# The E x E products of an attention and look-up feed-forward kernel, done by seven block products for eight

## The chip, the cores and the metric

The kernel runs on one core of one Trainium2 chip. The metric is the device time of one execution in microseconds (us), as the median of several runs. TensorE (PE) multiplies, VectorE (DVE) does elementwise work and the table look-ups, ScalarE (ACT) copies and does activations, GpSimd (POOL) and SyncE (SP) issue DMAs. Everything is fp32; one fp32 product appears in the trace as two MATMUL records, each with its weight load (PEld).

## The reference, cut to what matters

`x` is 2 x 2048 x 512, so there are B = 2 batches, S = 2048 tokens and E = 512 features.

```python
def attn(x, Wq, Wk, Wv, Wo):              # x is layer-normed
    q, k, v = x @ Wq, x @ Wk, x @ Wv
    qT, kT, vT = (swapaxes(t, 1, 2) for t in (q, k, v))   # b e s
    scores = einsum('bes,bfs->bef', qT, kT) / sqrt(16)    # 512 x 512 per batch
    o = einsum('bef,bfs->bes', softmax(scores), vT)
    return swapaxes(o, 1, 2) @ Wo

def ffn(x, lut, gate_idx, up_idx, down_idx):              # x is layer-normed
    gate, up = x @ lut[gate_idx].T, x @ lut[up_idx].T     # 1376 x 512 indices, 16 values
    return (silu(gate) * up) @ lut[down_idx].T

x = x + attn(layernorm(x), ...)
x = x + ffn(layernorm(x), ...)
```

The attention is over features, not tokens, so with n the normed tokens of a batch and G = n^T n (512 x 512), the scores are Wq^T G Wk / 4, and the output of the attention is n times M, where M = Wv A^T Wo and A is the softmax of the scores. Both G and M are 512 x 512 per batch.

## The kernel before, in words

The order of instructions on PE, ACT, DVE and SP is the order in which the program emits them; each engine's queue is worked off in that order, and an instruction that waits holds back all that were emitted after it on its engine. The program goes through these stages.

1. **Gram.** 8 chunks of 512 tokens (4 blocks of 128 each) are normed and multiplied into G of each batch (upper blocks only; `gram_mirror` fills the rest by PE transposes). Rows of n are stored in DRAM (`nd`), some here and some later (`n_stored`, one ACT pass and one DMA each).
2. **Eight E x E products.** For each batch: P1 = G Wk, scores S = Wq^T P1, softmax, T1 = A^T Wo, M = Wv T1. They come in the order p1_0, p1_1, s_0, s_1, t1_0, t1_1, m_0, m_1, where the last digit is the batch. `product` makes a result row block by row block: four blocks of 128 rows, each a bank of PSUM, filled by four products of 128 x 128 weights with 512 moving columns. ACT copies each bank out; for s, softmax runs on each row block by itself, with the maximum taken from PSUM on DVE and the exponent and the scaling by the reciprocal of the sum on ACT.
3. **y.** For each of 32 token blocks, `n_load` reads n back turned in 32 x 32 blocks, `n_turned` turns these blocks on DVE, `y_product` multiplies with M (4 products of 512 columns), and `side` adds the residual (DVE), takes the norm of the second layer (ACT), turns it by PE (`f_turned`) and, per two chunks, makes operand sums (`f_summed`).
4. **Gate and up** (`GateUp`): 11 blocks of 128 rows of weights by 4 pairs of chunks, each unit seven block products of Winograd's form (fourteen products of 512 columns).
5. **Down** (`Down`): 16 units of the same form with 256 moving columns.

The weights of stages 4 and 5 are looked up on DVE: a `Job` turns 128 x 1024 indices into values by some 20 steps of 0.4 to 1.3 us (bit tests, two-way choices with TENSOR_SCALAR, and COPY_PREDICATED). `gu0` to `gu10` are jobs for gate and up, `wd0` to `wd5` for down. The look-ups are spread over all other work by `pump(us)`, which emits so many us of steps (by the code's own costs, with a carried balance) at the place where it is called; the list `jobs` sets their order. A job `gu f` may start once unit f - 2 is through (its buffers come in twos).

Before, `pump` is called with 3.1 after each row block of p1, t1 and m, 2.2 in s, 0.3 in each y block and 0.8 between the products of stage 4. Tiles called `a0` to `a3`, `sq0`, `sq1` are 1 MB rooms that are reused: `a0` holds Wk, then Wo; `a1` holds Wq, then Wv^T.

Of the kernel before, what the change touches and what calls it, by code (L numbers as in the profile page):

```python
# [27 lines left out]

# [2 lines left out]

# [8 lines left out]
F32 = mybir.dt.float32  # L40
# [10 lines left out]
P = 128  # L51
H = 256
# [5 lines left out]
def tile_attn_ffn(  # L58
# [56 lines left out]
        return keep.tile([P, J, E], F32, tag=tag, name=name)  # L115

    wgu = tc.alloc_tile_pool(name="wgu", bufs=2)
    nlp = tc.alloc_tile_pool(name="nlp", bufs=1)
# [237 lines left out]
    def gram(c, j):  # L356
# [6 lines left out]
        for i in range(KB):  # L363
# [2 lines left out]
                start=c % CPB == 0 and j == 0, stop=c % CPB == CPB - 1 and j == J - 1,  # L366
            )

    gs = {}

    def gram_out(b):
# [38 lines left out]
    lut_pairs = lut_i.rearrange("p (k two) -> p k two", two=2)  # L410
    for c in range(1, NCH):
        for j in range(J):
            gram(c, j)
            if c + 1 < NCH and j < 2:
                for i in (2 * j, 2 * j + 1):
                    ln1[c + 1].stats(i, xc[c + 1][:, i, :])
                if j == 1:
                    ln1[c + 1].sqrt(0, J)
            elif c + 1 < NCH and j == 2:
                pump(0.6)  # L420
                ln1[c + 1].rest(0, J)
                pump(0.6)
            else:
                pump(1.9)
            if c == 1 and j == 2:
                nc.vector.tensor_tensor(
                    lut_x, lut_pairs[:, :, 0], lut_pairs[:, :, 1], ALU.bitwise_xor
                )
            if c == CPB and j == 1:
                gram_out(0)  # L430
            if c == CPB + 1 and j == 3:
                wk_sb = load_weight(wk, "a0", "wk_sb")
                wq_sb = load_weight(wq, "a1", "wq_sb")
            if c == CPB and j == 3:
                gram_mirror(0)

    def product(lhsT, rhs, name, by_slots=False):

        for m in range(KB):
            ps = bank(f"{name}_ps_{m}")  # L440
            for k in range(KB):
                cols = lhsT[:, k, m * P : (m + 1) * P]
                if by_slots:
                    cols = lhsT[:, k, :].rearrange("p (c m) -> p m c", m=KB)[:, m, :]
                nc.tensor.matmul(  # L445
                    ps, cols, rhs[:, k, :],
                    start=(k == 0), stop=(k == KB - 1),
                )
            yield m, ps

    def product_to(dest, lhsT, rhs, name, at=lambda m: None, by_slots=False):
        for m, ps in product(lhsT, rhs, name, by_slots):
            nc.scalar.copy(dest[:, m, :], ps)
            pump(3.1)
            at(m)
        return dest

    gram_out(1)
    to_store = iter([divmod(k, J) for k in range(STORED * J)])

    def n_stored(n=1):
        for c, j in itertools.islice(to_store, n):
            nc.sync.dma_start(nd[c, j], ln1[c].normed(j, xc[c][:, j, :]))

    p1 = [
        product_to(
            room("a2", "p1_0"), gs[0], wk_sb, "p1_0",
            lambda m: gram_mirror(1) if m == 1 else n_stored(),
        ),
        product_to(room("a3", "p1_1"), gs[1], wk_sb, "p1_1", lambda m: n_stored(1 + m % 2)),  # L470
    ]
    wo_sb = load_weight(wo, "a0", "wo_sb")
    att, last = [], None

    def softmax_end(a, m, sums, name):
        inv = small.tile([P, 1], F32, tag="inv", name=f"inv_{name}")
        nc.vector.reciprocal(inv, sums)
        nc.scalar.activation(a[:, m, :], a[:, m, :], AF.Copy, scale=inv)

    for b in range(B):  # L480
        a = room(f"sq{b}", f"a_{b}")
        for m, ps in product(wq_sb, p1[b], f"s_{b}"):
            pump(2.2)
            mx = small.tile([P, 1], F32, tag="mx", name=f"mx_{b}_{m}")
            nc.vector.reduce_max(mx, ps, axis=AX.X)
            nb = small.tile([P, 1], F32, tag="nb", name=f"nb_{b}_{m}")
            nc.vector.tensor_scalar_mul(nb, mx, -QK_SCALE)
            if last is not None:
                softmax_end(*last)
            sums = small.tile([P, 1], F32, tag="sums", name=f"sums_{b}_{m}")  # L490
            nc.scalar.activation(
                a[:, m, :], ps, AF.Exp, bias=nb, scale=QK_SCALE, accum_out=sums
            )
            last = a, m, sums, f"{b}_{m}"
            n_stored()
        att.append(a)
    pump(0.8)
    softmax_end(*last)
    wvT_sb = load_weight(wvT, "a1", "wvT_sb")
    t1 = [  # L500
        product_to(room(f"a{2 + b}", f"t1_{b}"), att[b], wo_sb, f"t1_{b}") for b in range(B)
    ]


    m_sb, nls, nTs, ys, xfs = [], {}, {}, {}, {}
    xb, xs = {}, {}

    def block(k):
        return xc[k // J][:, k % J, :]

    def n_load(h):

        if h < NBLK // 2:
            c, j = divmod(2 * h, J)
            nls[h] = nlp.tile([P, 2 * (P // Q), P], F32, tag="nl", name=f"nl_{h}", bufs=2)
            rows = nd[c, j : j + 2].rearrange("j (t b) e -> b (j t) e", b=Q)
            for i in range(KB):
                nc.sync.dma_start(nls[h][i * Q : (i + 1) * Q], rows[:, :, i * P : (i + 1) * P])

    def n_turned(k):  # L520

        if k < NBLK:
            n = P // Q
            nTs[k] = nlp.tile([P, KB, P], F32, tag="nT", name=f"nT_{k}", bufs=4)
            nc.vector.transpose(
                nTs[k].rearrange("p m (t b) -> p m t b", b=Q),
                nls[k // 2][:, n * (k % 2) : n * (k % 2) + n, :].rearrange(
                    "p t (a m) -> p m t a", a=Q
                ),
            )  # L530

    def y_product(k):
# [73 lines left out]
        if k % J == 0 and done in (1, 3):  # L606
            f_summed(done // 2)

    n_load(0)
    n_load(1)  # L610
    m_sb.append(product_to(room("sq0", "m_0"), wvT_sb, t1[0], "m_0", by_slots=True))
    m_sb.append(product_to(room("sq1", "m_1"), wvT_sb, t1[1], "m_1", by_slots=True))
    n_turned(0)
    n_turned(1)
    n_load(2)
# [9 lines left out]
    nlp.release()  # L625
    ffn = tc.alloc_tile_pool(name="ffn", bufs=1, reuse_waits="tile")


# [111 lines left out]
    def between():  # L740
        if todo:
            todo.pop(0)()
        else:
            pump(0.8)

    def tr(name):
        return psum("tr", name)
# [259 lines left out]
```

## Time and profile before

| | us |
|---|---|
| median of 3 runs | 1125.16 (1124.29 to 1125.23) |
| the profiled execution, device time | 1123.85 |
| its span, first to last instruction | 1121.8 |
| PE busy in the span | 1105.8 (99%) |
| DVE busy | 656.7 (59%) |
| ACT busy | 311.5 (28%) |
| the eight products, 80.26 to 190.78 | 110.5 |
| y, 190.78 to about 311 | 120 |
| gate and up, about 311 to 859 | 548 |
| down, 859 to the end | 263 |

The profiled execution is 2.05 us longer than its span; that remainder lies before the first and after the last instruction. The granted TensorE clock was 0.999. In the profile, a "group" is all instructions of one line, engine, operation and shape, with the total and the mean time of one; the chain is the sequence of work that ended last, followed back from the end. A mean duration of a MATMUL is longer than its share of PE's time, since matmuls overlap in the pipeline; PE's pace is read from the chain.

### The profile page before, as it was taken

Reading aid. Unit: us, or ns where it says so; the run is one execution under the profiler, and the core shown is the slowest. Engines: PE = TensorE matmul, PEld = TensorE weight load, DVE = VectorE, ACT = ScalarE, POOL = GpSimd, SP = SyncE. Lnnn points to the kernel's source line nnn. Section 1 sums busy time; section 2 is a strip of 40 time slices with the busy share of each in tenths; the row PEclk is TensorE's granted clock in tenths of the full one; section 3 lists DMA queues with packets and bytes.
Section 4 is the critical chain, followed back from the end, with each engine's and each line's share of the span. In section 5 each row is a group of like instructions: output and inputs, shape, how many; then the busy total and the mean of one; then the engine's idle time right before and its main releaser. Section 6 shows DMA issues by size and latency. Waiting matters only on the chain.

```text
span 1121.8 us, 9775 instructions
## 1 busy us (share of the span) xinstructions
PE 1105.8 (99%) x3388; PEld 630.4 (56%) x3388; DVE 656.7 (59%) x1191; ACT 311.5 (28%) x579; POOL 14.6 (1%) x31
## 2 busy tenths in 40 slices
PE   7999999999999999999999999999999999999998
PEld 4664446444444444444444444444437888888887
DVE  6896899566653847657566665856543344333341
ACT  4535622456562222222222222222221000000000
POOL 0000000000000000000000000000000000000000
PEclk9999999999999999999999999999999999999999
DMA  8253432444311111111211111111415453355420
GB/s 336 73 190 104 144 72 62 147 122 127 113 47 47 66 38 65 47 57 47 66 56 48 65 38 61 48 38 47 139 53 169 158 164 109 116 167 167 156 68 37
DMA packets 63232, 108.71 MB, mean 97 GB/s; under 512 B 5696, under 2 KB 22080, under 8 KB 61264
## 3 DMA queue, kind: packets, MB, share of 16 engines
q1 hardware_dynamic: 60992, 100.69, 26.6%
q0 software_dynamic: 2192, 7.41, 2.4%
q8 instruction: 26, 0.43, 0.2%
q14 instruction: 22, 0.18, 0.1%
HBM read 60.37 MB, written 47.71 MB: 96 GB/s over the span
## 4 chain that ended last, share of the span: by engine, by line
PE 98%; ACT 1%; DVE 0%; DMA 0%; issue 0%; ACTq 0%
PE a_g L637 27%; PE a_d L637 14%; PE c_g L637 13%; PE y L536 10%; PE c_d L637 7%; PE b_g L637 7%; PE gp L364 6%; PE b_d L637 4%; PE p_ps L445 2%; PE m_ps L445 2%; PE s_ps L445 2%; PE t_ps L445 2%; PE xt L560 1%; ACT xn_f L176 0%; DMA x<-in_x_dram 0%
## 5 line engine op out<-in xcount | busy, mean ns | idle before, releaser
L126 DVE TENSOR_TENSOR c<-c_g,u 128x512 f32<-128x512 f32 (+1 forms) x44 | 30.4, 690 | 178.3 <-PE c_g L637 178.3
L536 PE MATMUL y<-m,nT 128*128 128x512 f32 x256 | 114.0, 592 | 0.0
L637 PE MATMUL a_g<-xb,s 128*128 128x512 f32 (+1 forms) x176 | 82.8, 593 | 0.8 <-DVE c L126 0.8
L637 PE MATMUL a_g<-xT_a,s 128*128 128x512 f32 (+1 forms) x176 | 82.7, 592 | 0.0
L637 PE MATMUL a_g<-xb,w 128*128 128x512 f32 (+1 forms) x176 | 82.7, 592 | 0.0
L637 PE MATMUL c_g<-xb,w 128*128 128x512 f32 (+1 forms) x176 | 82.7, 592 | 0.0
L637 PE MATMUL b_g<-xb,w 128*128 128x512 f32 (+1 forms) x176 | 82.7, 592 | 0.0
L364 PE MATMUL gp<-xn_a 128*128 128x512 f32 (+3 forms) x256 | 71.2, 441 | 8.4 <-ACT xn_a L176 8.4
L536 PEld LDWEIGHTS y<-m,nT 128*128 128x128 f32 x256 | 46.8, 190 | 49.6 <-issue 49.5
L689 ACT ACTIVATE h<-h 128x512 f32<-128x512 f32 (+1 forms) x44 | 27.7, 630 | 156.9 <-DVE h L126 156.9
L364 PEld LDWEIGHTS gp<-xn_a 128*128 128x128 f32 x256 | 44.5, 193 | 34.9 <-issue 16.5
L637 PE MATMUL a_g<-xT_sq,s 128*128 128x512 f32 (+1 forms) x132 | 62.0, 592 | 0.0
L223 DVE TENSOR_SCALAR gu<-idx_gu,lut_x,lut_sb 128x1024 int32<-128x1024 int32 (+1 forms) x77 | 59.6, 790 | 0.0
L637 PEld LDWEIGHTS a_g<-xb,s 128*128 128x128 f32 (+1 forms) x176 | 32.9, 188 | 43.7 <-issue 37.7
L235 DVE COPY_PREDICATED gu<-b_gu,gu 128x1024 f32<-128x1024 int16 (+1 forms) x44 | 56.4, 1283 | 0.8
L637 PEld LDWEIGHTS b_g<-xb,w 128*128 128x128 f32 (+1 forms) x176 | 32.9, 188 | 42.0 <-issue 42.0
L637 PEld LDWEIGHTS c_g<-xb,w 128*128 128x128 f32 (+1 forms) x176 | 32.9, 188 | 41.6 <-issue 41.6
L637 PEld LDWEIGHTS a_g<-xb,w 128*128 128x128 f32 (+1 forms) x176 | 32.9, 188 | 41.5 <-issue 41.5
L637 PEld LDWEIGHTS a_g<-xT_a,s 128*128 128x128 f32 (+1 forms) x176 | 32.9, 188 | 41.5 <-issue 41.5
L637 PE MATMUL a_d<-dT,hs_a 128*128 128x256 f32 x224 | 56.2, 379 | 0.0
L235 DVE COPY_PREDICATED wd<-b_wd,wd 128x1024 f32<-128x1024 int16 (+1 forms) x42 | 51.1, 1217 | 1.1
L666 ACT COPY p<-a_g 128x512 f32<-128x512 f32 (+1 forms) x44 | 25.8, 586 | 84.1 <-PE a_g L637 84.1
(144 smaller groups left out, 1664.3 us busy)
## 6 DMA issues: line engine op xcount, KB each, us to landing
hd<-h SPq DMA_DIRECT2D x80, 256.0 KB, 2.0
h<-hd SPq DMA_DIRECT2D x40, 512.0 KB, 6.4
nd<-xn_a SPq DMA_DIRECT2D x32, 256.0 KB, 2.0
nl<-nd SPq DMA_DIRECT2D x64, 128.0 KB, 3.3
x1d<-x SPq DMA_DIRECT2D x8, 1024.0 KB, 4.1
r<-x1d SPq DMA_DIRECT2D x32, 256.0 KB, 4.2
out_dram<-r SPq DMA_DIRECT2D x32, 256.0 KB, 2.5
x<-in_x_dram SPq DMA_DIRECT2D x7, 1024.0 KB, 13.9
```

Source lines behind the costliest of these rows:

```text
L126: nc.vector.tensor_tensor(dest, a, b, ALU.add)
L223: vec.tensor_scalar(dest.bitcast(I32), idx, lut_x[:rows, k : k + 1], lut_i[:rows, at : at + 1], ALU.bitwise_and, ALU.bitwise_xor,)
L235: vec.copy_predicated(dest, masks[level - 1], t)
L364: nc.tensor.matmul(gp[b][i][:, i * P :], xn[:, i * P : (i + 1) * P], xn[:, i * P :], start=c % CPB == 0 and j == 0, stop=c % CPB == CPB - ...
L445: nc.tensor.matmul(ps, cols, rhs[:, k, :], start=(k == 0), stop=(k == KB - 1),)
L536: nc.tensor.matmul(ys[k], nTs[k][:, i, :], m[:, i, :], start=(i == 0), stop=(i == KB - 1))
L560: nc.tensor.transpose(ps[:, i * P : (i + 1) * P], xfs[k][:, i * P : (i + 1) * P], ident)
L637: nc.tensor.matmul(ps, lhsT, rhs, start=first and i == 0, stop=i == len(pairs) - 1, skip_group_check=not first,)
L666: nc.scalar.copy(self.p1, self.a)
L689: nc.scalar.activation(self.h0, self.h0, AF.Silu)
```

## The change

Each E x E product is now made by `Square`: the operands are cut into 2 x 2 blocks of 256 x 256, and the four result blocks come from seven block products in seven stages (in the order in which they are emitted: 11x11, S3xT3, S2xT2, 22xT4, S1xT1, 12x21, S4x22). A block product is 2 x 2 products of 128 x 128 weights by 256 moving columns; its two blocks of rows share one bank. Banks `u` (stages 0, 2, 4, 6) and `v` (stages 1, 3) are read out in the middle of their accumulation: stage 2 goes on adding to `u` after ACT has copied stage 0's sum, and so on. `left` and `right` give the four sums of an operand (one in place, three in new 256 KB tiles of the pool `sums`, ten in rotation), each one DVE operation of 128 x 512. `square` calls, after each stage, what the table `beside` lists for it, and then `pump(0.6)`.

The softmax runs on two row blocks at a time and reads the scores from SBUF. Wv^T is loaded by 16 DMAs that put its columns into another order, so that the weights of m are read without a stride; `n_load` now loads one block with four DMAs of 64 KB (before: two blocks with four DMAs of 128 KB), four blocks ahead, and takes its tiles, as `n_turned` does, from `sums` (before: from a pool of their own). Two places in Gram where `pump(1.9)` stood do the four sums of g_0 and of Wk instead. The order of look-up jobs changes, `pump` in y goes from 0.3 to 1.0, and in gate and up from 0.8 to 0.9.

```diff
-    jobs = [gu_job(0), gu_job(1)]
-    jobs += [down_job(i) for i in range(NPAIR + 1)]
-    jobs += [gu_job(f) for f in range(2, NFT)]
+    jobs = [gu_job(0), gu_job(1)] + [down_job(i) for i in range(NPAIR - 1)]
+    jobs += [gu_job(2), gu_job(3), down_job(NPAIR - 1), gu_job(4), gu_job(5), down_job(NPAIR)]
+    jobs += [gu_job(f) for f in range(6, NFT)]
...
+    def left(t, name, order=("S2", "S4", "S1")):
+        a11, a21 = t[:, 0:2, :H], t[:, 0:2, H:]
+        a12, a22 = t[:, 2:4, :H], t[:, 2:4, H:]
+
+        def s3():
+            for tag in order:
+                o.new(tag)
+            sub(a21, a11, a21)
+            o.update({"11": a11, "12": a12, "22": a22, "S3": a21})
+
+        o = Operand(name, [
+            s3, lambda: sub(o["S2"], a22, a21), lambda: sub(o["S4"], a12, o["S2"]),
+            lambda: add(o["S1"], o["S2"], a11),
+        ])
+        return o
...
+    class Square:
...
+        def mm(self, ps, a, b, first):
+            for m in range(2):
+                for k in range(2):
+
+                    nc.tensor.matmul(
+                        ps[:, m, :], self.a[a][:, k, m * P : (m + 1) * P], self.b[b][:, k, :],
+                        start=first and m == k == 0, stop=k == 1,
+                        skip_group_check=not (first and m == 0),
+                    )
...
+        def stages(self):
+            u = self.view("ea")
+            self.mm(u, "11", "11", True)
+            nc.scalar.copy(self.c11, u)
+            yield
+            v = self.view("ec")
+            self.mm(v, "S3", "T3", True)
+            nc.scalar.copy(self.c22, v)
+            yield
+            self.mm(u, "S2", "T2", False)
+            nc.scalar.copy(self.c21, u)
+            yield
+            self.mm(v, "22", "T4", False)
+            add(self.c21, v, self.c21)
+            yield
+            self.mm(u, "S1", "T1", False)
+            add(self.c22, u, self.c22)
+            yield
+            w = self.view("eb")
+            self.mm(w, "12", "21", True)
+            add(self.c11, w, self.c11)
+            yield
+            self.mm(u, "S4", "22", False)
+            nc.scalar.copy(self.c12, u)
+            yield
+
+    def square(a, b, dest, name, beside):
+
+        for i, _ in enumerate(Square(a, b, dest, name).stages()):
+            for op in beside.get(i, ()):
+                op()
+            pump(0.6)
...
+        def exp(self, h):
+            r = slice(2 * h, 2 * h + 2)
+            nc.vector.reduce_max(self.mx[:, r], self.a[:, r, :], axis=AX.X)
+            nc.vector.tensor_scalar_mul(self.nb[:, r], self.mx[:, r], -QK_SCALE)
+            for m in range(2 * h, 2 * h + 2):
+                nc.scalar.activation(
+                    self.a[:, m, :], self.a[:, m, :], AF.Exp, bias=self.nb[:, m : m + 1],
+                    scale=QK_SCALE, accum_out=self.sum[:, m : m + 1],
                 )
...
+        def end(self, h):
+            r = slice(2 * h, 2 * h + 2)
+            nc.vector.reciprocal(self.inv[:, r], self.sum[:, r])
+            for m in range(2 * h, 2 * h + 2):
+                nc.scalar.activation(
+                    self.a[:, m, :], self.a[:, m, :], AF.Copy, scale=self.inv[:, m : m + 1]
+                )
...
+    square(g[0], wk_ops, p1[0], "p1_0", {
+        1: [lambda: gram_mirror(1)], 2: [n_stored], 3: [n_stored], 4: g[1].todo[:2], 5: g[1].todo[2:],
+        6: [n_stored],
+    })
+    square(g[1], wk_ops, p1[1], "p1_1", {
+        0: [n_stored], 1: [n_stored], 2: wq_ops.todo[:2], 3: wq_ops.todo[2:],
+        4: [*p1_ops[0].todo[:2], n_stored], 5: p1_ops[0].todo[2:], 6: [n_stored],
+    })
...
+    square(wq_ops, p1_ops[0], att[0], "s_0", {
+        0: [n_stored], 1: [n_stored], 2: [*p1_ops[1].todo[:2], n_stored],
+        3: [*p1_ops[1].todo[2:], n_stored], 4: [lambda: soft[0].exp(1)],
+        5: [lambda: soft[0].end(1)], 6: [n_stored],
+    })
+    square(wq_ops, p1_ops[1], att[1], "s_1", {
+        0: [lambda: soft[0].exp(0)], 1: [lambda: soft[0].end(0)], 2: [n_stored],
+        3: [*wo_ops.todo[:2], n_stored], 4: [*wo_ops.todo[2:], lambda: soft[1].exp(1)],
+        5: [*att_ops[0].todo[:2], lambda: soft[1].end(1)], 6: att_ops[0].todo[2:],
+    })
+
+    wvT_sb = room("a1", "wvT_sb")
+    for k in range(KB):
+        for i in range(KB):
+            nc.sync.dma_start(
+                wvT_sb[:, k, :].rearrange("p (m c) -> p m c", m=KB)[:, :, i * Q : (i + 1) * Q],
+                wvT[k * P : (k + 1) * P, i * P : (i + 1) * P].rearrange("p (m a) -> p m a", a=Q),
             )
...
+    square(att_ops[0], wo_ops, t1[0], "t1_0", {
+        0: [lambda: soft[1].exp(0)], 1: [lambda: soft[1].end(0)], 2: att_ops[1].todo[:2],
+        3: att_ops[1].todo[2:], 4: [n_stored], 5: [n_stored],
+    })
+    square(att_ops[1], wo_ops, t1[1], "t1_1", {
+        3: wv_ops.todo[:2], 4: [*wv_ops.todo[2:], t1_ops[0].todo[0]], 5: t1_ops[0].todo[1:],
+    })
...
+    square(wv_ops, t1_ops[0], m_sb[0], "m_0", {2: t1_ops[1].todo[:2], 3: t1_ops[1].todo[2:]})
+    square(wv_ops, t1_ops[1], m_sb[1], "m_1", {
+        0: [lambda: n_load(0)], 3: [lambda: n_turned(0), lambda: n_load(1)],
+        6: [lambda: n_turned(1), lambda: n_load(2), lambda: n_load(3)],
+    })
     for k in range(NBLK):
         n_turned(k + 2)
-        if k % 2:
-            n_load((k + 1) // 2 + 2)
+        n_load(k + 4)
         y_product(k)
         if k >= 1:
             side(k, bank)
-        pump(0.3)
+        pump(1.0)
...
-            pump(0.8)
+            pump(0.9)
```

`right` is like `left`: T3 in place, then T2, T4 and T1, one DVE operation each.

More of the change, by code (lines that the diff above doesn't have):

```diff
@@ L31 @@
-import itertools
 from contextlib import ExitStack
@@ L117, in tile_attn_ffn @@
     wgu = tc.alloc_tile_pool(name="wgu", bufs=2)
-    nlp = tc.alloc_tile_pool(name="nlp", bufs=1)
+    sums = tc.alloc_tile_pool(name="sums", bufs=10)
     gub = tc.alloc_tile_pool(name="gub", bufs=1, side="right")
@@ L367, in gram, with __init__, new, right @@
             )
+    class Operand(dict):
+        def __init__(self, name, todo):
+            self.name, self.todo = name, [lambda op=op: op() for op in todo]
+        def new(self, tag):
+            self[tag] = sums.tile([P, 2, H], F32, tag="e", name=f"{tag}_{self.name}")
+            return self[tag]
+    def left(t, name, order=("S2", "S4", "S1")):
[11 more added lines that the diff above has]
+        return o
+    def right(t, name, order=("T2", "T4", "T1")):
+        b11, b12 = t[:, 0:2, :H], t[:, 0:2, H:]
+        b21, b22 = t[:, 2:4, :H], t[:, 2:4, H:]
+        def t3():
+            for tag in order:
+                o.new(tag)
+            sub(b12, b22, b12)
+            o.update({"11": b11, "21": b21, "22": b22, "T3": b12})
+        o = Operand(name, [
+            t3, lambda: add(o["T2"], b12, b11), lambda: sub(o["T4"], b21, o["T2"]),
+            lambda: sub(o["T1"], b22, o["T2"]),
+        ])
+        return o
     gs = {}
@@ L410, in tile_attn_ffn @@
     lut_pairs = lut_i.rearrange("p (k two) -> p k two", two=2)
+    ahead = []
     for c in range(1, NCH):
@@ L422, in tile_attn_ffn @@
                 pump(0.6)
+            elif ahead:
+                for op in ahead[:4]:
+                    op()
+                del ahead[:4]
             else:
@@ L433, in tile_attn_ffn @@
                 wq_sb = load_weight(wq, "a1", "wq_sb")
+                wk_ops = right(wk_sb, "wk")
+                ahead += wk_ops.todo
             if c == CPB and j == 3:
                 gram_mirror(0)
[L437 to L447, printed above, removed]
-                )
-            yield m, ps
@@ L451, in product_to @@
[L451 to L456, printed above, removed]
-    gram_out(1)
[L459 to L471, printed above, removed]
@@ L472, in tile_attn_ffn @@
-    wo_sb = load_weight(wo, "a0", "wo_sb")
[L473 to L492, printed above, removed]
-            )
-            last = a, m, sums, f"{b}_{m}"
-            n_stored()
-        att.append(a)
@@ L497, in tile_attn_ffn, with __init__, view @@
-    pump(0.8)
[L498 to L505, printed above, removed]
+                g_ops = [left(gs[0], "g_0")]
+                ahead += g_ops[0].todo
+    class Square:
+        def __init__(self, a, b, dest, name):
+            self.a, self.b, self.name = a, b, name
+            self.c11, self.c12 = dest[:, 0:2, :H], dest[:, 0:2, H:]
+            self.c21, self.c22 = dest[:, 2:4, :H], dest[:, 2:4, H:]
+        def mm(self, ps, a, b, first):
[6 more added lines that the diff above has]
+                    )
+        def view(self, tag):
+            return bank(f"{tag}_{self.name}").rearrange("p (m h) -> p m h", m=2)
+        def stages(self):
[23 more added lines that the diff above has]
+            yield
@@ new lines, in square, with n_stored, __init__, cols @@
+    def square(a, b, dest, name, beside):
+        for i, _ in enumerate(Square(a, b, dest, name).stages()):
+            for op in beside.get(i, ()):
+                op()
+            pump(0.6)
+    to_store = iter([divmod(k, J) for k in range(STORED * J)])
+    def n_stored():
+        c, j = next(to_store)
+        nc.sync.dma_start(nd[c, j], ln1[c].normed(j, xc[c][:, j, :]))
+    class Softmax:
+        def __init__(self, a, name):
+            self.a, self.name = a, name
+            def cols(tag):
+                return small.tile([P, KB], F32, tag=tag, name=f"{tag}_{name}")
+            self.mx, self.nb, self.sum, self.inv = (cols(t) for t in ("mx", "nb", "sum", "inv"))
+        def exp(self, h):
[6 more added lines that the diff above has]
+                    scale=QK_SCALE, accum_out=self.sum[:, m : m + 1],
+                )
+        def end(self, h):
[5 more added lines that the diff above has]
+                )
@@ new lines, in tile_attn_ffn @@
+    gram_out(1)
+    g = [g_ops[0], left(gs[1], "g_1")]
+    wq_ops = left(wq_sb, "wq", ("S2", "S1", "S4"))
+    p1 = [room(f"a{2 + b}", f"p1_{b}") for b in range(B)]
+    p1_ops = [right(p1[b], f"p1_{b}") for b in range(B)]
+    assert not ahead
+    square(g[0], wk_ops, p1[0], "p1_0", {
[6 more added lines that the diff above has]
+    })
@@ new lines, in tile_attn_ffn @@
+    wo_sb = load_weight(wo, "a0", "wo_sb")
+    wo_ops = right(wo_sb, "wo")
+    att = [room(f"sq{b}", f"a_{b}") for b in range(B)]
+    soft = [Softmax(att[b], f"{b}") for b in range(B)]
+    att_ops = [left(att[b], f"att_{b}", ("S1", "S2", "S4")) for b in range(B)]
+    square(wq_ops, p1_ops[0], att[0], "s_0", {
[3 more added lines that the diff above has]
+    })
@@ new lines, in tile_attn_ffn @@
+    wv_ops = left(wvT_sb, "wv", ("S2", "S1", "S4"))
+    t1 = [room(f"a{2 + b}", f"t1_{b}") for b in range(B)]
+    t1_ops = [right(t1[b], f"t1_{b}", ("T1", "T2", "T4")) for b in range(B)]
+    square(att_ops[0], wo_ops, t1[0], "t1_0", {
[5 more added lines that the diff above has]
+    })
@@ L506, in tile_attn_ffn @@
+    nls, nTs, ys, xfs = {}, {}, {}, {}
     xb, xs = {}, {}
@@ L509, in block, with n_load @@
         return xc[k // J][:, k % J, :]
[L511 to L516, printed above, removed]
+    def n_load(k):
+        if k < NBLK:
+            c, j = divmod(k, J)
+            nls[k] = sums.tile([P, P // Q, P], F32, tag="e", name=f"nl_{k}")
+            rows = nd[c, j].rearrange("(t b) e -> b t e", b=Q)
             for i in range(KB):
-                nc.sync.dma_start(nls[h][i * Q : (i + 1) * Q], rows[:, :, i * P : (i + 1) * P])
+                nc.sync.dma_start(nls[k][i * Q : (i + 1) * Q], rows[:, :, i * P : (i + 1) * P])
     def n_turned(k):
         if k < NBLK:
-            n = P // Q
-            nTs[k] = nlp.tile([P, KB, P], F32, tag="nT", name=f"nT_{k}", bufs=4)
+            nTs[k] = sums.tile([P, KB, P], F32, tag="e", name=f"nT_{k}")
             nc.vector.transpose(
                 nTs[k].rearrange("p m (t b) -> p m t b", b=Q),
-                nls[k // 2][:, n * (k % 2) : n * (k % 2) + n, :].rearrange(
-                    "p t (a m) -> p m t a", a=Q
-                ),
+                nls[k].rearrange("p t (m a) -> p m t a", a=Q),
             )
@@ L607, in side @@
             f_summed(done // 2)
[L609 to L615, printed above, removed]
+    m_sb = [room(f"sq{b}", f"m_{b}") for b in range(B)]
+    square(wv_ops, t1_ops[0], m_sb[0], "m_0", {2: t1_ops[1].todo[:2], 3: t1_ops[1].todo[2:]})
[3 more added lines that the diff above has]
+    })
     for k in range(NBLK):
         n_turned(k + 2)
-        if k % 2:
-            n_load((k + 1) // 2 + 2)
+        n_load(k + 4)
         y_product(k)
@@ L622, in tile_attn_ffn @@
             side(k, bank)
-        pump(0.3)
+        pump(1.0)
     pps.release()
-    nlp.release()
+    sums.release()
     ffn = tc.alloc_tile_pool(name="ffn", bufs=1, reuse_waits="tile")
@@ L743, in between @@
         else:
-            pump(0.8)
+            pump(0.9)
     def tr(name):
```

## The prediction

> **What bounds the kernel now.** I read first the page's busy times, then the chain in order of time, then windows over the eight products, then the groups by shape.
>
> ```profile
> PE 1105.8 (99%) x3388; PEld 630.4 (56%) x3388; DVE 656.7 (59%) x1191; ACT 311.5 (28%) x579; POOL 14.6 (1%) x31
> ```
>
> PE is never idle for long, so only less PE time, or new waits of PE, can move the end. The chain gives PE's pace (start, length, count of records):
>
> ```profile
> 80.26 6.87 PE p_ps L445 x16
> 87.13 0.66 PE gt L383 x6
> 87.78 20.60 PE p_ps L445 x48
> 108.38 27.47 PE s_ps L445 x64
> 135.85 27.47 PE t_ps L445 x64
> 163.32 27.47 PE m_ps L445 x64
> 865.93 4.75 PE a_d L637 x22
> ```
>
> The eight products are one unbroken run from 80.26 to 190.8. A record with 512 columns takes 27.47 / 64 = 0.429 us; one with 256 columns (last row, the down stage) takes 4.75 / 22 = 0.216 us. The windows over p1, s, t1 and m (columns: PE, PEld, DVE, ACT, POOL busy) show what else is there:
>
> ```profile
> 80.30:108.40 28.10, 28.10 (x71) 12.76 (x70) 19.03 (x24) 12.11 (x21) 0.72 (x1) 1.00 0.26 86
> 108.40:135.80 27.40, 27.40 (x65) 12.09 (x65) 21.11 (x38) 18.27 (x32) 0.72 (x1) 1.00 0.39 134
> 135.80:163.30 27.50, 27.50 (x66) 12.31 (x65) 26.79 (x35) 7.16 (x12) 0.72 (x1) 1.00 0.45 111
> 163.30:190.80 27.50, 27.50 (x66) 19.64 (x65) 27.12 (x31) 6.15 (x10) 1.65 (x3) 1.00 0.09 27
> ```
>
> DVE is full in the last two rows, with look-ups that nobody waits for. After the change work that PE does wait for goes into the same queue.
>
> **What is removed on PE.** A product is 16 matmuls, 32 records: 32 x 0.429 = 13.73 us. Seven block products are 28 matmuls, 56 records of 256 columns: 56 x 0.216 = 12.09 us. Eight times 1.64 is 13.1 us. This needs the weight load to stay hidden behind 0.216 us:
>
> ```profile
> L637 PE MATMUL a_d<-dT,hs_a 128*128 128x256 f32 x224 | 56.2, 379 | 0.0
> L637 PEld LDWEIGHTS a_d<-dT,hs_a 128*128 128x128 f32 x224 | 42.4, 189 | 6.0
> L445 PEld LDWEIGHTS m_ps<-t,wvT_sb 128*128 128x128 f32 x64 | 19.7, 308 | 7.9 <-issue 0.2
> ```
>
> The down stage loads 128 x 128 weights in 189 ns beside matmuls paced at 216 ns, and 16 units of it run without a gap; the new products have the same shape. The strided load of m (308 ns) would not fit, and the new order of Wv^T's columns takes that stride away. [...]
>
> **What is added on DVE and ACT.** In the eight products, at the spacing of back-to-back operations (a 128x512 add lasts 0.68 and the next starts 0.60 to 0.61 later):
> 40 operand sums (the eight of g_0 and Wk lie in Gram, in place of 3.8 us of look-ups): 40 x 0.605 = 24.2 us.
> 24 additions from PSUM (three a product): 24 x 0.61 = 14.6 us.
> Four maxima of 128x1024: the 128x512 one is 0.69, and adds of 512 and 1024 elements (0.68, 1.22) say 0.53 more, 1.22 each, with negation 1.4: 5.5 us.
> Look-ups: 56 x 0.6 = 33.6 us of the code's cost, times 1.045 (a job `wd` costs 16.6 by the code and 17.3 by the rows): 35.1 us. Before it was 92.8.
>
> With two transposes this is 81.6 us, against 96.7 us of PE: it fits on the whole, but it comes in bunches, and the leash is short. Before, a late DVE or ACT had eight banks of slack. Now stage 4 may not start on `u` before ACT copied stage 2, stage 6 not before DVE's `add(c22)` of stage 4, stage 3 not before ACT copied stage 1: one stage, 8 x 0.216 = 1.73 us, of slack each time.
>
> **The dense stretch.** From DVE's addition in stage 3 of s_1 to its `add(c22)` in stage 4 of t1_0, on which stage 6 waits, DVE gets: five additions (3.1), four sums of Wo, four of att_0, four of att_1 (12 x 0.605 = 7.3), two maxima with negation (2.8), eight pumps (5.0): 18.2 us. PE has nine stages there, 15.5 us. So 2.7 us are missing even if DVE never waits. It does wait: the reciprocal of a softmax half stands behind its two exponents on ACT (0.67 us and a read of the sum, 0.68 apart, so 1.4), and ACT's scalings stand ahead of the copies that free `u` and `v`. In t1_0, stages 0 and 1, only one pump step of about 0.6 covers this, so 1 us more; and a step of 1.3 us (COPY_PREDICATED) just ahead of a wanted addition, seen from PE, costs half of itself twice: 1.3 us. I take 5 us here. From s_0 to s_1 the other halves meet less DVE work, but ACT has five `n_stored` of 0.8 us, the table load for the exponent (1.28 us, idle-hidden before) and the scalings: 1.2 us. In p1_1, t1_1, m_0 and m_1 two sums and a look-up step stand ahead of `add(c22)`: about 0.45 us each, 1.8. Sum 8.0 us. The lower bound is the 2.7 us of pure shortage. The upper one takes each mean duration in full instead of the spacing (20.1 us in the stretch, 4.6 missing, two waits of 1.7, so 8.0), 2 us for s, and 0.7 for each of six lesser products: 14 us, all of the gain. I take 8.0, nearer the middle, because the rows show DVE's operations overlapping at their ends.
>
> **What is moved.** Look-ups leave the products (59.2 us of cost) and Gram (3.8), and 22.4 go to y. In y, PE needs 3.87 us a block (3.44 for y, 0.43 for the turn), DVE 1.1 (transpose) + 0.77 (residual) + 0.25 (norm) + 1.05 = 3.2: it fits, and the transpose runs two blocks ahead of its product, so that the 4.9 us of `f_summed` at blocks 16 and 24 find slack. The last 40.6 go to gate and up, where `pump(0.9)` allows 25.2 per block of weights and a job costs 18.3, so the rest is worked off in about six blocks. DVE's window there:
>
> ```profile
> 427.00:475.00 48.00, 48.00 (x114) 21.21 (x113) 30.31 (x44) 12.89 (x21) 1.06 (x2) 1.00 0.16 54
> ```
>
> 30.3 of 48 us become about 39; the additions there have at least two stages (3.4 us) of slack, so 0. Only at block 4 are some 2 us of steps issued in one go, since wd4 stands before gu4; the products already in PE's queue cover it. If that cover is gone it costs those 2 us. POOL's index loads follow the jobs and are hundreds of us early. The start of y: tile nT_1 needs a load that SP can issue only after stage 4 of m_1, because its room holds a sum of Wv until then; 4 issues of 0.45 and 3.3 to land, then 1.1, end about 3 us after m_1, and y_1 starts 3.4 after it. Just in time; I put 0.5 us there. The 16 passes of `n_stored` stay 16. `n_load`'s 64 more issues (0.45 each, 1.8 a block of 3.87) have room on SP; the x1d stores behind them are early.
>
> **The load of Wv^T.** 16 DMAs with 128-byte pieces, 8192 of them, issued when stage 5 of s_1 has read Wq's room, wanted by DVE in stage 3 of t1_1: 1.7 + 12.1 + 5 + 6.9 = 25.7 us later, and the stage after it covers some 1.7 more. No row shows 128-byte pieces.
>
> ```profile
> nl<-nd SPq DMA_DIRECT2D x64, 128.0 KB, 3.3
> wvT_sb<-in_wvT_dram SPq DMA_DIRECT2D x1, 1024.0 KB, 7.0
> ```
>
> The low bound is the plain load, 7.0. `nl` has 256 pieces of 512 bytes a DMA, issued every 0.45 us (median) to 1.28 (longest): 1.8 to 5.0 ns a piece, so 14.4 to 41 us, and 3.3 to land: 18 to 44. I take 18, the median row: hidden. [...]
>
> **The sum.** 1123.85 (profiled) - 13.1 + 8.0 + 0.5 = 1119.25. The profiled execution lies 1.3 us under the median, so the median to come is 1125.16 - 4.6 = **1120.6**. A difference under 0.2% (2.25 us) I count as none.
>
> **The rivals.**
> *DVE keeps up* (0.12): the waits overlap and only the shortage of 2.7 us stays: 1125.16 - 13.1 + 2.7 + 0.5 = 1115.3. For it: DVE's 81.6 us are 84% of PE's 96.7. Against: the bunch in s_1 and t1_0.
> *DVE and ACT give it all back* (0.16): 14 us of waits, 1126.6; with 11 and more it is no difference. For it: every softmax half is a chain DVE, ACT, DVE, ACT in queues that also hold the copies.
> *Wv^T comes late* (0.22, slower): one mechanism. It decides from 27.4 us after its issue; each us more holds DVE in t1_1, with `add(c22)` behind it, and PE in stage 6. From 34 us on the kernel is slower by over 0.2%; at 40 us it is 1120.6 + 12.6 = 1133.2. For it: the bound of 44 us, and that no row shows such pieces. Against: the median row.
> That 256-column products don't run at 0.216 us I leave out: 16 units of the down stage show them.
>
> **How the numbers follow.** The forecast, 5 to 10.8 us of waits (1117.6 to 1122.9), has 0.50. Faster is this and the first rival, 0.62; same is the second, 0.16; slower the third, 0.22. The range from 1115.0 to 1130.0 leaves out half of the first rival's lower side (0.05) and half of the third (0.11).
>
> **What would show it.** Right: 448 records of 256 columns in place of 256 of 512, p1 at about 25 us a pair with the turns, PE waits on DVE and ACT of 8 us, most in s_1 and t1_0; y from about 186; DVE above 80% busy in the products and about 39 of 48 us in the early blocks of gate and up, with no wait of PE there. Wrong: PE idle in t1_1 behind a DMA; waits spread evenly over all eight products; a pace other than 0.216; PE waiting in y or in gate and up.

## The result, and the profile after

The changed kernel takes 1121.16 us (median of 6 runs, 1119.73 to 1121.98); the one before takes 1125.04 in the runs beside it. The ratio is 0.9966, 95% interval 0.9954 to 0.9979, so 0.34% faster; the forecast was 1120.6.

The profiled execution took 1121.98 us with a span of 1119.9. It is a poor match for the one of before (1123.85, faster than all six of that kernel's runs in the comparison): the two differ by 1.9 us, the medians by 3.9. Most of the reason stands in the first 16 us, whose code is the same; it comes up again at the end. What follows is therefore read stage by stage. Busy times of the page first:

```profile
PE 1098.1 (98%) x3580; PEld 660.4 (59%) x3580; DVE 683.8 (61%) x1251; ACT 315.4 (28%) x587; POOL 14.7 (1%) x31
```

PE is busy 7.7 us less, and DVE, which has the operand sums and the additions to do, 27 us more. The windows over the pairs p1, s, t1 and m (columns as before: length, then PE, PEld, DVE, ACT, POOL busy with counts, PE's clock, DMA):

```profile
81.52:107.01 25.49, 25.10 (x120) 21.81 (x119) 15.02 (x22) 10.55 (x20) 0.00 (x0) 1.00 0.17 63
107.01:132.43 25.42, 24.71 (x113) 21.05 (x112) 20.65 (x34) 16.81 (x29) 0.73 (x1) 1.00 0.42 147
132.43:162.80 30.37, 26.90 (x113) 22.14 (x112) 22.22 (x36) 12.22 (x23) 0.00 (x0) 0.94 0.26 51
162.80:187.63 24.83, 24.44 (x113) 21.20 (x112) 18.86 (x28) 4.69 (x8) 0.72 (x1) 1.00 0.27 74
```

The lengths add up to 106.1 us, 4.4 less than before (110.5). A pair without any wait would take 24.2 (56 x 2 records of 0.216), and m comes within 0.7 of it; p1 has 0.66 us of transposes inside. t1 takes 30.4, and PE's clock there is 0.94. PE's records in order of time show t1_0 from its first stage on (start, length, what; in brackets the idle time named and what ended it; eight records at pace are 1.73 us apart from start to start):

```profile
132.43 1.89 PE L499 MATMUL ea_t<-wo_sb,a 128*128 128x256 f32 x8
134.61 1.97 PE L499 MATMUL ec_t<-wo_sb,a 128*128 128x256 f32 x8 [0.29 <-DVE a L122]
137.64 1.99 PE L499 MATMUL ea_t<-T_wo,S_att 128*128 128x256 f32 x8 [1.07 <-ACT t L511]
141.70 2.56 PE L499 MATMUL ec_t<-T_wo,a 128*128 128x256 f32 x8 [2.07 <-ACT t L515]
144.05 3.06 PE L499 MATMUL ea_t<-T_wo,S_att 128*128 128x256 f32 x8
146.95 1.89 PE L499 MATMUL eb_t<-wo_sb,a 128*128 128x256 f32 x8
```

Stage 1 waits for DVE's sum of att_0, stage 2 for ACT's copy of stage 0, stage 3 for ACT's copy of stage 1. The starts of stages 1 to 5 are late against the pace by 0.45, 1.30, 2.33, 0.62 and 1.17 us, 5.9 in all. The last two have no wait in front of them: 0.10 of the 0.62 is PE's restart (behind waits after which the matmuls are not slow, the next start comes 1.83 us later for 1.73: 105.18 to 107.01 in p1_1 behind 0.39 us, 125.42 to 127.25 in s_1 behind 0.36, 173.72 to 175.55 in m_0 behind 0.39), and the rest is matmuls that are slow themselves. The chain shows what stood before the longest wait (start, length, engine, what):

```profile
135.59 0.72 DVE wd L222
136.31 0.60 DVE S_att L122
136.91 0.60 DVE S_att L125
137.51 0.72 DVE wd L222
138.24 1.14 DVE mx L560
...
139.40 0.18 DVE nb L561
...
139.66 1.52 ACT a L563 x4
141.18 0.48 ACT t L515
...
141.70 1.35 PE ec_t L499 x5
```

The maximum of the softmax's second half belongs to stage 0 of t1_0 (over at 134.3), but DVE comes to it at 138.24, behind two look-up steps and two sums. Its input is late as well: ACT's last copy of s_1 ends at 137.1, because it stands behind scalings that waited for DVE's reciprocal of 135.19. ACT can do the exponents only after the maximum, and the copy that PE wants (L515) stands behind these. DVE's shortage reaches PE through ACT. And PE's clock in the windows around it (length, PE busy, clock):

```profile
134.00:141.70 7.70, 4.28 (x18) 1.00 0.68 108
141.70:143.00 1.30, 1.30 (x6) 1.00 0.00 0
143.00:146.00 3.00, 3.00 (x9) 0.50 0.35 129
```

PE was busy 4.28 of 7.70 us, and from 143 on, with work in hand, its granted clock is 0.50 for 3.4 us (0.80 between 146 and 147). That costs 0.57 us on stage 3's records (2.56 in the chain, for the 1.99 of eight records behind a wait at full clock) and 1.12 on stage 4's (2.85 for 1.73): 1.7 in all. Waits and restarts make up the other 4.2 of the 5.9.

After the products nothing is slower up to the first block of weights: y takes 120.85 us to the first product of gate and up, 120.84 before. In gate and up DVE is busier, as foreseen (a window of 48 us, in it 36.99 of DVE where before it had 30.31):

```profile
423.50:471.50 48.00, 48.00 (x113) 21.24 (x112) 36.99 (x52) 13.76 (x22) 2.15 (x4) 1.00 0.18 64
```

There is one wait, at the start of weight block 4, in PE's records in order of time:

```profile
507.67 1.98 PE L752 MATMUL c_g<-xb,w 128*128 128x512 f32 x4 [0.79 <-DVE w L122]
```

So the two profiled runs compare like this: Gram 1.4 us later to its end (chance, see below), products 4.4 shorter, y 0, gate and up 1.05 longer (0.79 of wait, the other 0.26 PE's restart): 1.9 us less.

### The profile page after: what moved, and what is told of

Same layout as the page of the kernel before. It is cut to its first block, busy times and chain, and to the rows that moved or that the text cites. A ratio compares the mean times of both kernels' runs of the same rounds, so it can differ in the third digit from the quotient of the medians.

```text
span 1119.9 us, 10385 instructions
## 1 busy us (share of the span) xinstructions
PE 1098.1 (98%) x3580; PEld 660.4 (59%) x3580; DVE 683.8 (61%) x1251; ACT 315.4 (28%) x587; POOL 14.7 (1%) x31
## 4 chain that ended last, share of the span: by engine, by line
PE 93%; DVE 4%; ACT 2%; issue 0%; DMA 0%; DVEq 0%; ACTq 0%
PE a_g L752 27%; PE a_d L752 14%; PE c_g L752 13%; PE y L653 10%; PE c_d L752 7%; PE b_g L752 7%; PE gp L363 6%; PE b_d L752 4%; PE xt L677 1%; PE ea_p L499 1%; PE ea_m L499 1%; PE ea_t L499 1%; PE ec_p L499 1%; PE ec_t L499 1%; PE ec_s L499 0%; DVE mx L560 0%
## 5 line engine op out<-in xcount | busy, mean ns | idle before, releaser
L125 DVE TENSOR_TENSOR c<-c_g,u 128x512 f32<-128x512 f32 (+1 forms) x44 | 30.4, 691 | 142.0 <-PE c_g L752 135.2
L125 DVE TENSOR_TENSOR r<-r,a_d 128x256 f32<-128x256 f32 x32 | 13.5, 421 | 54.8 <-PE a_d L752 54.8
```

The costliest lines, as they stand in the source:

```text
L125: nc.vector.tensor_tensor(dest, a, b, ALU.add)
```

## The experiments

Theory: in s_1 and t1_0 DVE has more work than PE gives it time for, and the softmax steps that come late from DVE hold ACT's copies; both together are the waits. Rivals: the softmax's chain alone, whatever DVE holds; or DVE's load alone; or something in the new form that hits all products alike, such as reading banks in the middle of accumulation; or the look-ups' spreading is what gains.

**No look-ups in the bunch.**

```diff
+    DENSE = {("s_1", i) for i in range(3, 7)} | {("t1_0", i) for i in range(4)}
-            pump(0.6)
+            if (name, i) not in DENSE:
+                pump(0.6)
...
-        pump(1.0)
+        pump(1.15)
```

> Edit: no pump in stages 3 to 6 of s_1 and 0 to 3 of t1_0 (eight of 0.6); y pumps 1.15 instead of 1.0. Theory (DVE has 18.2 us of work in the bunch against 15.5 us of PE, and the late softmax steps hold ACT's copies): 5 us of DVE work leave the bunch, the eight products take about 101 us instead of 106.1, TensorE's clock is not halved behind the wait in t1_0, and the time is about 1116. Rival (the softmax's chain of DVE, ACT, DVE, ACT alone sets the waits, whatever else is in DVE's queue): products stay at 105 to 106, time about 1121.

Measured: 1117.35 us, ratio 0.9938 (0.9921 to 0.9955). The products take 101.8 us, t1 26.2 instead of 30.4, and the clock stays at 1.00. In t1_0 the wait of stage 1 is gone, and those of stages 2 and 3 become 0.99 and 1.06:

```profile
136.31 1.99 PE L499 MATMUL ea_t<-T_wo,S_att 128*128 128x256 f32 x8 [0.99 <-ACT t L511]
139.36 1.99 PE L499 MATMUL ec_t<-T_wo,a 128*128 128x256 f32 x8 [1.06 <-ACT t L515]
```

That the chain alone sets the waits falls: 4.3 us go with 4.8 us of look-ups. Of the 4.3, 1.7 are the clock and 1.6 waits of t1_0. The last 1.0 lies in t1_1 and m_0, behind the bunch: other look-up steps now stand in front of the additions there (in m_0 no step at all, where the changed kernel has one of 1.3 us). Two waits on ACT remain, and those of s_1 are what they were.

**The softmax's halves one stage later.**

```diff
-        0: [lambda: soft[0].exp(0)], 1: [lambda: soft[0].end(0)], 2: [n_stored],
+        1: [lambda: soft[0].exp(0)], 2: [lambda: soft[0].end(0), n_stored],
...
-        0: [lambda: soft[1].exp(0)], 1: [lambda: soft[1].end(0)], 2: att_ops[1].todo[:2],
-        3: att_ops[1].todo[2:], 4: [n_stored], 5: [n_stored],
+        1: [lambda: soft[1].exp(0)], 2: [lambda: soft[1].end(0)], 3: att_ops[1].todo[:2],
+        4: [*att_ops[1].todo[2:], n_stored], 5: [n_stored],
```

(The sums of att_1, which need the halves, come a stage later with them.)

> Edit: the second half of each softmax is called one stage later (exponents behind the copy of stage 1, scalings behind the copy of stage 2), all look-ups as they are. Theory (the copies that free u and v stand behind exponents that wait for DVE): the waits of stages 2 and 3 in s_1 and t1_0 go, some 3 to 4 us, products about 102.5 to 103, time about 1117.5; what DVE lacks in the bunch stays. Rival (only DVE's total in the bunch counts): products stay within 1 us of 106, time about 1121.

Measured: 1117.81 us, ratio 0.9941 (0.9926 to 0.9956); products 102.65 us, with all look-ups in place. The wait of stage 3 in t1_0 is gone, in s_1 too; that of stage 2 (1.07) stays, and two small ones of 0.34 and 0.29 us come in stages 4 and 6. On ACT the copy L515 now starts at 137.14, right behind L511, and no longer behind the exponents (139.32), which come as late in the stage as before. So the order on ACT's queue matters beside DVE's load. Of the 3.5 us gained in the products, 1.7 are again the clock, which is not halved here (stages 3 and 4 of t1_0 take 1.89 and 1.99 us, for 2.56 and 3.06 in the changed kernel), and 1.8 are waits.

**No softmax at all.** The edit takes the calls of `exp` and `end` out of the tables.

> Leaves the softmax out (maxima, exponents, sums, scalings); look-ups and sums stay. Theory: DVE's bunch loses 3 us and ACT's copies wait for nothing, products about 100 us. Rival (the look-ups and sums alone overfill DVE's bunch): products 103 or more. If reading a bank in the middle of its accumulation cost anything by itself, it would still show, at all eight products alike.

Measured (a single run): products 99.2 us, time 1114.83. What is left are two waits of 0.39 us, in p1_1 and m_0 (0.65 each with the restart), and 0.3 and 0.2 us in t1_1 and t1_0. The other four products run at pace; the new form as such costs next to nothing beyond its 97.4 us (96.7 and the 0.66 of transposes). The rivals that look-ups and sums alone make the waits, and that reading a bank in the middle of accumulation costs something, fall as well.

**The look-ups spread as before.**

```diff
-            pump(0.6)
+            pump(1.65)
...
-        pump(1.0)
+        pump(0.3)
...
-            pump(0.9)
+            pump(0.8)
```

(and the old list of jobs)

> Undoes one part: the look-ups are spread as before (1.65 per stage in the products, which is the old 92.8 over 56 stages, 0.3 in y, 0.8 in gate and up, the old order of jobs). Theory: DVE has about 82 - 35 + 97 = 144 us of work in the products and PE waits for it, products 135 to 145 us, time about 1152. Rival (look-ups never hold PE, they only fill idle time): products about 106, time 1121.

Measured (a single run): 1152.49 us, products 138.3, in which DVE is busy 127.6 us (92%). PE's list of waits names DVE where before there was nothing, or at most 0.4 us (what waited, on what, us in total, times, longest):

```profile
PE ea_s L499 <- DVE a L125: 6.5, 2, 4.4
PE ea_m L499 <- DVE m L125: 6.0, 2, 5.4
PE ea_p L499 <- DVE p L125: 5.8, 1, 5.8
```

Without room on DVE the change would have cost 28 us (1124.49 beside it) instead of gaining 4. Of the 41 us that the products take beyond their 97.4, about 30 are waits with their restarts and 11 the slow records behind five of them, which I put down to the halved clock seen above (eight records take 3.50 to 3.78 us for 1.99, and the clock of this run is 0.986 on the mean).

**The old products, with the look-ups spread later.**

```diff
-            pump(3.1)
+            pump(1.05)
...
-        pump(0.3)
+        pump(1.0)
...
-            pump(0.8)
+            pump(0.9)
```

(2.2 becomes 1.05 too, the single 0.8 behind s goes; the new list of jobs)

> One part alone: the products of before (512 columns, row block by row block), with the look-ups spread as in the changed kernel (1.05 per row block, which is 4.2 a product; 1.0 in y, 0.9 in gate and up, the new order of jobs). Theory (the spreading gains nothing by itself, it only empties DVE): products 110.5 us as before, plus 0.8 us of wait at weight block 4, time 1125 to 1126. Rival (the gain of the change comes from the look-ups being spread better): time about 1121.

Measured: 1125.44 us against 1124.26, ratio 1.001 (1.0001 to 1.0019). Products 110.5, the wait of 0.8 us at weight block 4 is there. The spreading gains nothing alone.

**All three edits.** The two above that helped, and, to get rid of the 0.8 us, gu4 ahead of wd4:

```diff
-    jobs += [gu_job(2), gu_job(3), down_job(NPAIR - 1), gu_job(4), gu_job(5), down_job(NPAIR)]
+    jobs += [gu_job(2), gu_job(3), gu_job(4), down_job(NPAIR - 1), gu_job(5), down_job(NPAIR)]
```

> Edits together: no pump in the bunch (y 1.15), softmax halves a stage later, and gu4 before wd4 in the list of jobs. Theory: the waits of the bunch are one shortage seen from two sides, so the two savings (4.3 and 3.5 us in the products) overlap: products 99 to 100 us; the wait of 0.8 us at the start of weight block 4 goes; time 1114.5 to 1115. Rival (the two edits remove different waits and add up): products 98 us or less, time under 1113.5.

Measured: 1119.56 us, ratio 0.9957 (0.9944 to 0.9971), slower than either edit alone. The products take the 99.9 us that the theory gave, but not for its reason. The two edits together save 6.2 us where the sum of the two is 7.7, and the 1.5 between them is about the halved clock (1.7), which each had removed by itself. Without it the waits saved are 2.6, 1.8 and, together, 4.5: they add up, as the rival had it.

The loss is in the list of jobs, and the edit was a mistake. Block 4 (from 497.6) has no wait any more, but gu5 now stands behind wd4, and the wait of 0.8 us comes at block 5; and gu6 has its last step done 2.7 us too late for block 6 (chain: start, length, engine, what):

```profile
547.97 0.35 DVE w L122
548.36 1.98 PE c_g L755 x4
...
596.38 1.22 DVE w L234
597.64 3.78 PE a_g L755 x4
```

The job gu4 may start only once unit 2 is through. In this run DVE does no look-up step from 431.5 to 451.0, and wd4, which had its place there, comes later and pushes gu5 and gu6 back.

**All four.** As before, and two of Wo's sums earlier:

```diff
-        5: [lambda: soft[0].end(1)], 6: [n_stored],
+        5: [lambda: soft[0].end(1)], 6: [*wo_ops.todo[:2], n_stored],
...
-        3: [*wo_ops.todo[:2], n_stored], 4: [*wo_ops.todo[2:], lambda: soft[1].exp(1)],
+        3: [*wo_ops.todo[2:], n_stored], 4: [lambda: soft[1].exp(1)],
```

> As the one before, and the first two sums of Wo move from stage 3 of s_1 to stage 6 of s_0, the others from 4 to 3. Theory: 1.2 us more leave DVE's bunch, products about 98.5 us, time about 1114. Rival (the bunch is no longer short): the same as the run before within 0.5 us.

Measured: 1116.89 us, ratio 0.9934 (0.9921 to 0.9946). The products take 98.7 us, 1.2 less than without this edit, as expected; the time misses by the same wait of 2.7. But the median is 2.7 us under that of the run before, and the two profiled runs are 4.3 apart. The clock behind that one wait differs. First the run with three edits, then with four (length, PE busy, clock):

```profile
598.00:604.00 6.00, 6.00 (x8) 0.51 0.00 0
```

```profile
597.00:603.00 6.00, 6.00 (x16) 1.00 0.00 0
```

In six us PE did 8 records in one and 16 in the other, behind a wait of 2.66 us in both. Eight records from the wait on take 6.60 us (597.64 to 604.24) and 3.54 (596.40 to 599.94): 3.1 us, which with the 1.2 make the 4.3. The profiled run with three edits is the slowest of its five.

**Three edits, the old list of jobs, and pump 1.0 in gate and up.** By the code's counts 0.9 leaves 1.6 us of steps to be issued in one go at block 4 and 1.0 leaves none (with my list it is block 5, and more at block 6). In the trace of the changed kernel four sums of the job stand together there on DVE, from 506.4 to 507.9, and PE waits for the third.

```diff
-            pump(0.9)
+            pump(1.0)
```

> Edits: no pump in the bunch (y 1.15), softmax halves a stage later, two sums of Wo in s_0, and pump 1.0 instead of 0.9 in gate and up with the list of jobs as in the changed kernel. By the code's counts no look-up step is then left to be issued in one go ahead of a weight block. Theory: products 98.7 us as in the run with four edits, no wait of 0.8 or 2.7 us in gate and up, time about 1114. Rival (a fuller DVE in gate and up makes PE wait there): named waits of PE in gate and up grow, time 1116 or more.

Measured: 1112.43 us, ratio 0.9891 (0.9876 to 0.9907): 1.1% under the kernel before, and 8.6 us under the changed kernel on the same chip. The products take 98.7 us (7.4 less than in the changed kernel), and the wait at the weight blocks is gone (1.05 less); the windows of gate and up from 330 to 570 show PE busy in all of it with DVE up to 39 of 48 us:

```profile
522.00:570.00 48.00, 48.00 (x113) 21.28 (x112) 39.36 (x63) 13.83 (x22) 2.13 (x4) 1.00 0.18 66
```

**Wv^T in plain pieces.**

```diff
-        for i in range(KB):
-            nc.sync.dma_start(
-                wvT_sb[:, k, :].rearrange("p (m c) -> p m c", m=KB)[:, :, i * Q : (i + 1) * Q],
-                wvT[k * P : (k + 1) * P, i * P : (i + 1) * P].rearrange("p (m a) -> p m a", a=Q),
-            )
+        nc.sync.dma_start(wvT_sb[:, k, :], wvT[k * P : (k + 1) * P, :])
```

(This kernel leaves out the reordering of the columns that m's weights need; its operations keep their shapes.)

> Only edit: Wv^T is loaded by four DMAs with 2 KB pieces and its columns stay in their old order, so that the reordering of the columns is left out. Theory (the load by 128-byte pieces is through long before it is wanted): products 106 us as in the changed kernel, time 1121; DVE loses at most the 0.5 us that it spends on the waits for sixteen DMAs. Rival (the load holds DVE in t1_1): products 1 us shorter or more, time under 1120.

Measured: 1119.58 us, ratio 0.9958 (0.9944 to 0.9972); products 105.1, 1.0 shorter. Taken by my own bounds this would be the rival. The profile speaks against it: in the changed kernel the sixteen loads land by 141.3 us and DVE comes to them at 158.19, straight behind its addition of 157.58, as it does here (155.62 behind 155.01). What differs is the clock. The same waits of 1.07 and 2.07 us stand in t1_0 of both, but behind them the clock is 1.00 here and halved in the changed kernel, whose second run on this chip comes next (windows of PE: length, busy, clock; first the plain load, then the changed kernel):

```profile
141.00:143.00 2.00, 2.00 (x11) 1.00 0.00 0
143.00:145.00 2.00, 2.00 (x11) 1.00 0.71 262
```

```profile
141.00:143.00 2.00, 2.00 (x6) 0.53 0.00 0
143.00:145.00 2.00, 2.00 (x7) 0.61 0.49 182
```

The clock is worth 1.7 us, and 0.6 comes back as a wait in stage 6 of t1_0 (0.37 named, with the restart): together about the 1.0. Why the clock did not drop is not settled.

**The changed kernel again**, on the chip of the last two:

> The changed kernel itself beside the others on this chip: 1121 us, and again a halved TensorE clock behind the wait in t1_0 if that wait and not chance sets it off.

Measured: 1121.05 us, ratio 0.9967 (0.9955 to 0.998); products 106.1 us, the same waits to 0.01 us, and again a halved clock behind them, worth 1.7 us (eight records in 3.46 and 2.15 us, where 1.99 and 1.89 are usual).

## Why the prediction was right

**PE's gain.** Foreseen 13.1 us by 0.216 us a record. Eight records are 1.73 us apart wherever nothing waits, and the run without a softmax comes to 99.2 us with 97.4 of pure pace. Right. The weight loads stay hidden (190 ns a load in m, which was 308). With the load not hidden, 448 records of 0.216 + 0.190 would have made the products 182 us, an estimate from these two numbers; they took 106.1.

**What comes back.** Foreseen 8.0 us, measured 8.7 (106.1 less 97.4, of which 0.66 are the transposes). By place: s_0 to s_1 1.2, measured 1.2 (0.51 and 0.72); the single late additions 1.8, measured 1.6 (0.65 in p1_1, 0.3 in t1_1, 0.65 in m_0, none in m_1); the bunch 5.0, measured 5.9. In the bunch the step was right in its cause, as the first two experiments show, and off in two details. I had the wait that counts in stage 6, behind `add(c22)`; it came in stages 1 to 3, most of it by way of ACT's copies. ACT's copies were named, but at a price of 1 us. And only 4.2 of the 5.9 are waits and restarts; 1.7 are the halved clock, which no term had. The waits were put 0.8 too high and the clock at nothing, and it is luck that these two errors partly cancel. DVE's work in the products was put too high: 76.8 us busy of 106.1, which is 72%, for the 81.6 and the 80% that were to be a sign of being right. At this load it is not DVE's total that makes the waits, but where its steps stand.

**What was moved.** y costs nothing, as foreseen; the 0.5 us for its start were not needed. The 2 us of steps in one go at weight block 4 I put at 0, under the cover of products in PE's queue; the cover lacks 0.8 us (with the restart 1.05). The term was named and priced, and its cover was the wrong part. DVE's 39 of 48 us in the early blocks came as 30.3 to 40.3, from window to window.

**Wv^T.** Foreseen 18 us to land, with bounds of 7 and 44; measured 10.4 from the first issue, and wanted only at 158.2:

```profile
wvT_sb<-in_wvT_dram SPq DMA_DIRECT2D x16, 64.0 KB, 2.3
```

Sixteen issues from 130.9 to 139.0, about 0.5 us each, and 2.3 to land. The 18 us by my median row were too high: a piece of 128 bytes comes to 1.0 ns of issue here (512 of them in 0.505 us) where that row has 1.8 for one of 512 bytes (256 in 0.45). The rival that put the slower side there had 0.22 and no ground in what was measured.

**The sum.** -13.1 + 8.7 in the products, + 1.05 in gate and up: -3.35, against a difference of the medians of -3.9; run to run the start of Gram alone moves by more than that gap. Against the forecast's -4.6 the terms came out 1.25 higher (the products' waits and clock 0.7, weight block 4 1.05, y's start -0.5); that the forecast misses the median by only 0.6 is in part the luck of that gap.

## What to carry to other kernels

PE's work was shortened here by adding operand sums, and the price was set where DVE's and ACT's new steps bunch up (5.9 of 8.7 us in t1_0), not by their total (DVE was busy in 72% of the products' time). In such a change count a stretch's queue against PE's time there, and look where the copy that PE wants stands in the queue. Emitting a step that waits one stage later, behind that copy, gained nearly as much here as taking 4.8 us of filler out of DVE's queue (3.5 and 4.3 us in the products, 1.7 of each by the clock), and both together, with two sums moved ahead of the bunch and a slightly steeper filler rate later, gave 1.1% instead of 0.34%. Savings on waits that share a slow clock must not be added as they stand (7.7 us by the sum, 6.2 in the run). Filler work that is owed by a deadline is best checked by adding up the code's own counts before each deadline.

## What the runs showed of the hardware

**The clock after short waits.** In t1_0 PE was busy 4.28 of 7.70 us, and then ran at a granted clock of 0.50, from 1.3 us after it had full work again. The half clock lasted 3.4 us (143.0 to 146.4), and 3.4 again in the second run of the same kernel, worked out, with the clock taken as either half or full, from its 0.53 and 0.61 over two windows of 2 us. A wait of 2.66 us at a weight block was followed by 6.8 us of it in one kernel (worked out in the same way from 0.88 over 4 us and 0.51 over 6) and by none in the next (1.00 over both). In the run with the look-ups spread as before, the five waits of 2.7 to 5.8 us were each followed by eight records that took 3.5 to 3.8 us for 1.99, and the one of 2.1 us was not. The shortest wait that the half clock followed here is the one of 2.07 us in t1_0 (2.06 in the second run), with one of 1.07 us ahead of it; behind the same two waits the run with the plain load shows 1.00. Why the clock falls behind one wait and not behind the same wait in another run, no run here tests.

**The start.** PE's first records of 512 columns last 1041 to 1221 ns, up to about 10 us in the run of before and up to about 13 in the profiled run after, then 592 to 595; the clock column reads 1.00 in that time. The beginning of the products lies between 79.99 and 81.79 us over the twelve profiled runs, although the code up to 50 us is the same. These 1.8 us are of the size of the spread of one kernel's times (2.25 for the changed kernel's six), and more than several of the effects above; phases of the profile settle what single times can't.
